# Four places in the lead-in of a graph attention kernel: tables, norms, a list of edges and an average are emitted later

## The chip, the cores and the metric

The kernel runs on one core of one Trainium2 chip. The metric is device time in microseconds (us) of one execution, as the median of several runs. A core has TensorE (matmul; the profile writes PE, and PEld for its weight loads), VectorE (DVE), ScalarE (ACT), GpSimd (POOL) and SyncE (SP, which here only issues DMAs). Each engine works through its own list of instructions in order; semaphores make one wait for another.

## The reference

A layer of graph attention with a residual and a layer norm. There are 16 batches of 1024 rows of 512 numbers, one adjacency matrix for all, 8 heads of 64. Cut to what matters:

```
q = x @ Wq + bq;  k = x @ Wk + bk;  v = x @ Wv + bv      # split in 8 heads
scores = q . k / sqrt(64) + (1 - adj) * -1e9
out = softmax(scores) . v;  y = layernorm(x + out @ Wo + bo)
```

`adj` is 0 or 1 and sparse: a row has an edge to few others, and low row numbers have many more than high ones. A row without any edge gets the mean of all v, since all its scores are then equally low.

## The kernel before, in words

**Rows are sorted by their number of edges.** In a lead-in the kernel ranks the 1024 rows, and then treats them in eight tiles of 128. For each tile it gathers, key by key, the row of k and v of each query's own next key (a "block", 128 queries by one key), so nothing is computed for absent edges. A tile t has OWN[t] blocks of that sort. Tiles 6 and 7, the rows with most edges, have besides BLOCKS[t] blocks of packed surplus edges, which a matmul with a 0/1 matrix (`sums`) adds to their queries. The function `edges(t)` makes the list of a tile's surplus: it gathers the tile's rows of `adj` (L635, on GpSimd, 128 by 1024, `codes`), multiplies them with the numbers of the places (L640), takes the greatest eight again and again (L659, L661), computes offsets through a matmul (L676), and looks for the list's entries by matmuls with 0/1 matrices (L701 to L724). `REST_FROM` says at which place of the schedule each starts.

**Tables of merged tiles.** From batch 2 on, the rows with fewest edges of two batches share one tile. `more_ranks` loads the tables for those, called `others`, by 19 small DMAs on SP (L539, L543), computes from them the rows asked for and their keys on VectorE (L552 to L578), and then squares Wq by heads on ScalarE (L583), for a bound that a final check uses. `lookups` turns keys into places, one small gather on GpSimd a step (L596), and reads the keys of `others` last.

**The fronts.** For each pair of tiles of each batch the fronts compute q, k and v from x. x is gathered (L1004), transposed (`pxT`, L751), copied by ScalarE (`xT`), and multiplied with Wq (`pq`, L793) and, in a scheme of Strassen's kind with seven products for eight, with the blocks of Wk and Wv (L950; `x`, `pp`, `z`). VectorE and ScalarE put the parts together: `e` (L963), `w` (L966), `g` (L969), k and v (L829, L973, L978, L982), `q` (L824). SP writes q, k and v to DRAM, from where GpSimd gathers them by rows. When all of a batch's v are there, `add_v` has summed them (`vsum`, L854 and L857) and `mean_pe` multiplies the sum by 1/1024 (`pm`, L861); ScalarE copies the row and SP writes it behind the batch's rows (L867). Only after that are the batch's k and v gathered.

**Attention.** For block n: gather of k and v (`kvg`, L1263), product with q (`qk`, L1284) and its sums by heads (`s`, L1288) on VectorE, exponential (L1299) and weighing of v (L1312) on ScalarE, adding up on VectorE (L1328) or TensorE (`sum`). A finished tile is divided by its sum, transposed (`poT`), multiplied with Wo (`po`), gets residual and layer norm, and is scattered to the output.

**The order is written out by hand.** One loop runs over places n, from −39 (the lead-in) to the last block, and emits the instructions for all engines. At place n it emits the product for block n + 4, gathers up to block n + 8, what was put off until n by `later` (`plan`), then what `later_last` put off, then TensorE's units as a budget of time ("credit") allows (2.0 us a place from −13 to −1, before that 3.3), and at the end one piece of each running preparation (`prep`: generators, each `yield` of which ends a place). In that part a unit of the fronts comes first, then what is in `urgent`, then more units. `edges(7)` starts at −24, `lookups` at −17, `more_ranks` at −12, `edges(6)` at −9, `bias_setup` at −8. PSUM tiles named `fill` have four buffers, shared by `pq`, `pp`, `pxT`, `pm`, `poT`, `po` and the preparations. `bias_setup` brings the biases into place (L396 to L405), adds bv times Wo to bo (`pb`, L419 and L421), and takes the greatest norms of bk and bq (L408 to L414), which are needed only by the check, at the start of the last batch.

```
if 0 <= n + 4 < total:
    products(n + 4)
...
for fn in plan.pop(n, ()):
    fn()
...
preps += prep.pop(n, [])
preps = [g for g in preps if next(g, True) is None]
```

Of the kernel before, what the change touches and what calls it, by code (L numbers as in the profile page):

```python
# [10 lines left out]
F32 = mybir.dt.float32  # L11
# [3 lines left out]
OP = mybir.AluOpType  # L15
# [16 lines left out]
KG_BUFS, Q_BUFS, QT_BUFS, PV_BUFS, Y_BUFS = 8, 5, 3, 5, 6  # L32
# [26 lines left out]
ADJ_AT = {-36: (0,), -35: (1, 2), -34: (3, 4), -33: (5,), -32: (6, 7)}  # L59
CHECKS_AT = -27  # L60
BIAS_AT = -8
MORE_RANKS_AT = -12
LOOK_FROM = -17
REST_FROM = {7: -24, 6: -9}

PRODUCT = 0.86
SUM = 0.87
# [6 lines left out]
P = 128  # L74
# [103 lines left out]
def kernel(  # L178
# [36 lines left out]
    nc = tc.nc  # L215
    B, N, D = x.shape
    HD = D // HEADS
    NPAIR = D // P
# [22 lines left out]
    W = {}  # L241
# [3 lines left out]
    bo_bc = const.tile([P, D], F32, name="bo_bc")  # L245
    flag = const.tile([1, 1], I32, name="flag")

    def broadcast(t, v):
        nc.scalar.dma_start(t, bass.AP(tensor=v.tensor, offset=v.offset, ap=[[0, P], [1, D]]))
# [4 lines left out]
    with ExitStack() as main:  # L254
        one = main.enter_context(tc.tile_pool(name="one", bufs=1))
        work = main.enter_context(tc.tile_pool(name="work", bufs=1))
# [4 lines left out]
        def fill_psum(name):  # L261
            return psum.tile([P, HALF], F32, tag="fill", name=name, bufs=4)
# [67 lines left out]
        def kv_of(b):  # L330

            if b < PAIRED_FROM:
                return solo_rows[b], 0
            rows = pair_views[b // 2 % 2][b % 2]
            return (rows, N + 1) if b % 2 else (rows[0:N + 1, :], 0)
# [58 lines left out]
        def bias_setup():  # L394
            pb = fill_psum("pb")
            nc.tensor.transpose(pb[:, 0:2 * NPAIR], bias_rows, ident[:2 * NPAIR, :2 * NPAIR])  # L396
            nc.tensor.transpose(pb[:, 2 * NPAIR:3 * NPAIR], bv_rows, ident[:NPAIR, :NPAIR])
            bk_bc = work.tile([P, D], F32, tag="y", name="bk_bc", bufs=Y_BUFS)
            broadcast(bk_bc, bk)
            yield  # L400
            nc.vector.tensor_copy(bias_qk, pb[:, 0:2 * NPAIR])
            bv_col = one.tile([P, NPAIR], F32, name="bv_col")
            nc.vector.tensor_copy(bv_col, pb[:, 2 * NPAIR:3 * NPAIR])
            bvb = work.tile([P, NPAIR, P], F32, tag="y", name="bvb", bufs=Y_BUFS)
            nc.vector.tensor_copy(bvb, bv_col[:, :, None].to_broadcast([P, NPAIR, P]))  # L405
            yield
            n4 = small.tile([P, NPAIR], F32, name="bk_norms", bufs=1)
            nc.vector.tensor_tensor(bk_bc, bk_bc, bk_bc, op=OP.mult)  # L408
            nc.vector.tensor_reduce(n4, bk_bc.rearrange("p (h d) -> p h d", d=P), axis=AX.X, op=OP.add)
            nc.vector.tensor_reduce(bk_norm, n4, axis=AX.X, op=OP.max)  # L410
            n8 = small.tile([P, HEADS], F32, name="bq_norms", bufs=1)
            nc.vector.tensor_tensor(bk_bc, bq_bc, bq_bc, op=OP.mult)
            nc.vector.tensor_reduce(n8, bk_bc.rearrange("p (h d) -> p h d", d=HD), axis=AX.X, op=OP.add)
            nc.vector.tensor_reduce(bq_norm, n8, axis=AX.X, op=OP.max)  # L414
            for _ in range(4):
                yield
            pb = fill_psum("pb3")
            for c in range(NPAIR):
                nc.tensor.matmul(pb, bvb[:, c, :], W["o"][:, c, :], start=(c == 0), stop=(c == NPAIR - 1))  # L419
            yield  # L420
            nc.vector.tensor_tensor(bo_bc, pb, bo_bc, op=OP.add)  # L421

        def bias_pieces():

            r = work.tile([P, D], F32, tag="y", name="bo_rest", bufs=Y_BUFS)
            nc.vector.tensor_copy(bo_3, bo_bc)
            nc.vector.tensor_tensor(r, bo_bc, bo_3, op=OP.subtract)
            yield  # L430
            nc.vector.tensor_copy(bo_3[32:33, :], r[32:33, :])
            nc.vector.tensor_copy(bo_3[64:65, :], r[64:65, :])
            nc.vector.tensor_tensor(r[64:65, :], r[64:65, :], bo_3[64:65, :], op=OP.subtract)
            nc.vector.tensor_copy(bo_3[64:65, :], r[64:65, :])
            yield
            st = small.tile([P, 1], F32, name="two", bufs=1)
            nc.vector.tensor_tensor(st, ident[:, 0:1], ident[:, 32:33], op=OP.add)
            nc.vector.tensor_tensor(three, st, ident[:, 64:65], op=OP.add)

        now, plan, rest, urgent, known, waiting, combined = [0], {}, {}, [], [], [], []  # L440

        def later(k, fn):
            plan.setdefault(now[0] + k, []).append(fn)
# [143 lines left out]
        def lookups():  # L587
            at = NS + NK
            groups = [[NS + own[t] + i for i in range(OWN[t])] for t in range(NT)]
            groups += [[first[t] + i for i in range(BLOCKS[t])] for t in range(len(SHORT), NT)]  # L590
            groups.append(list(range(at, at + 4)))
            for i, group in enumerate(groups):
                while i >= NT and i < len(groups) - 1 and len(SHORT) + i - NT not in listed:
                    yield
                for g in group:
                    nc.gpsimd.indirect_dma_start(  # L596
                        out=found_place[:, g:g + 1], out_offset=None, in_=place_of,
                        in_offset=bass.IndirectOffsetOnAxis(ap=key_row[:, g:g + 1], axis=0), bounds_check=N, oob_is_err=False,
                    )
                    yield  # L600
                lo, hi = group[0], group[-1] + 1

                def copy(lo=lo, hi=hi):
                    if lo == at:
                        nc.vector.scalar_tensor_tensor(
                            found_place[:, at + 1:at + 3], shifts[0].to_broadcast([P, 2]), N + 1.0, found_place[:, at + 1:at + 3],
                            op0=OP.mult, op1=OP.add,
                        )
                        nc.vector.scalar_tensor_tensor(
                            found_place[:, at + 3:], shifts[1], N + 1.0, found_place[:, at + 3:], op0=OP.mult, op1=OP.add  # L610
                        )
                    nc.vector.tensor_copy(place_row[:, lo:hi], found_place[:, lo:hi])
                    looked.append(lo)

                later(3, copy)
# [3 lines left out]
        def checks():  # L619
            for t in range(NT):  # L620

                a = ADJ[t]
                nc.scalar.activation(a, a, AF.Square, bias=neg_one, scale=2.0)
                nc.scalar.activation(a, a, AF.Square, bias=neg_one, accum_out=check[:, t:t + 1])
                yield
# [184 lines left out]
        def pair(b, j):  # L810
# [21 lines left out]
            def out_v(i, p):  # L832
                nc.scalar.copy(KV[b, tt[i]][:, D:], p)
                send(i)

            def send(i):
                assert b < PAIRED_FROM or gathered[0] >= start[max(0, b // 2 * 2 - 2)]
                kv = KV[b, tt[i]]
                rows, base = kv_of(b)
                for lo, hi in ((0, LONE), (LONE + P, 2 * P)) if b and tt[i] == 0 else ((tt[i] * P - (LONE if b and tt[i] == 1 else 0), None),):  # L840
                    hi = lo + P if hi is None else hi
                    part = slice(0 if lo % P == 0 or hi - lo == P else LONE, P if hi - lo == P or lo else LONE)
                    later(1, lambda lo=lo, hi=hi, part=part: nc.sync.dma_start(rows[base + lo:base + hi, :], kv[part, :]))
                R["sent"] = R.get("sent", 0) + 1
                if R["sent"] == 2:
                    later(1, add_v)
                    if j == NT // 2 - 1:
                        later(2, lambda: urgent.append(mean_pe))

            def add_v():  # L850
                kv = [KV.pop((b, t))[:, D:] for t in tt]
# [129 lines left out]
            def out_v0():  # L981
                nc.vector.tensor_tensor(KV[b, tt[0]][:, D:], R["z"], R["w"], op=OP.add)  # L982
                send(0)
# [223 lines left out]
        start = [min(n for n, block in enumerate(blocks) if block[0] == b) for b in range(B)] + [len(blocks)]  # L1207
# [266 lines left out]
        prep = {}  # L1474
        for t, n in REST_FROM.items():
            prep.setdefault(n, []).append(edges(t))
        prep.setdefault(BIAS_AT, []).append(bias_setup())
        prep.setdefault(CHECKS_AT, []).append(checks())
        preps = [loads(), ranks()]
        prep.setdefault(start[B - 1] + 8, []).append(guard())  # L1480
        prep.setdefault(start[1], []).append(bias_pieces())
        prep.setdefault(MORE_RANKS_AT, []).append(more_ranks())
        prep.setdefault(LOOK_FROM, []).append(lookups())
        with tc.manual_schedule():
# [21 lines left out]
            while n < total or plan or rest or urgent or done or finishing or spilled or lone_tiles or not guarded:  # L1506
# [6 lines left out]
                elif n in start:  # L1513

                    b = start.index(n)
# [110 lines left out]
```

## Time and profile before

| | |
|---|---|
| median of 3 runs | 1864.6 us (1860.19 to 1864.85) |
| the profiled execution, its own time | 1867.63 us |
| its span from first to last instruction | 1865.9 us |
| busy share of the span: TensorE, VectorE, ScalarE, GpSimd | 97%, 90%, 84%, 66% |
| mean granted clock of TensorE | 0.988 |
| DMA | 553.82 MB, mean 297 GB/s |

A page of the profile gives for each engine its busy time, and for each group of instructions the line, the operation, output<-inputs by their names in the program, and the count. In a timeline a row is start, length (both us), engine, line, operation, and in brackets the idle time of that engine before it and what ended it. Rows of one line that follow each other are merged, so that "x4" is four instructions; a float32 matmul has two records. In a list of waits a row gives who waited for what: sum in us, number, longest. The granted clock is 1.00 where TensorE ran at full speed.

### The profile page before, as it was taken

Reading aid. Unit: us, or ns where it says so; the run is one execution under the profiler, and the core shown is the slowest. Engines: PE = TensorE matmul, PEld = TensorE weight load, DVE = VectorE, ACT = ScalarE, POOL = GpSimd, SP = SyncE. Lnnn points to the kernel's source line nnn. Section 1 sums busy time; section 2 is a strip of 40 time slices with the busy share of each in tenths; the row PEclk is TensorE's granted clock in tenths of the full one; section 3 lists DMA queues with packets and bytes.
Section 4 is the critical chain, followed back from the end, with each engine's and each line's share of the span. In section 5 each row is a group of like instructions: output and inputs, shape, how many; then the busy total and the mean of one; then the engine's idle time right before and its main releaser. Section 6 shows DMA issues by size and latency. Waiting matters only on the chain.

```text
span 1865.9 us, 25322 instructions
## 1 busy us (share of the span) xinstructions
PE 1812.4 (97%) x5150; PEld 879.3 (47%) x5150; DVE 1686.2 (90%) x3462; ACT 1564.6 (84%) x6184; POOL 1237.3 (66%) x1154
## 2 busy tenths in 40 slices
PE   7989999999999999999999999999999999999995
PEld 3434444454444545444444445444544444444442
DVE  6888789999989999999999999999999999997885
ACT  3627778988889898999889898999899998987785
POOL 1367775777665776767766676677766767665774
PEclk9999999999999999999999999999999999999997
DMA  7357787998888899998998988998989999889993
GB/s 283 116 174 221 234 305 244 306 333 314 314 284 300 286 325 331 329 320 304 322 332 299 341 304 306 346 317 312 342 293 320 322 350 328 306 320 315 355 307 115
DMA packets 195431, 553.82 MB, mean 297 GB/s; under 512 B 33162, under 2 KB 33182, under 8 KB 195266
## 3 DMA queue, kind: packets, MB, share of 16 engines
q0 software_dynamic: 113600, 373.64, 59.1%
q1 hardware_dynamic: 78590, 172.65, 24.8%
q10 hardware_dynamic: 3076, 5.82, 0.9%
q14 instruction: 122, 1.00, 0.2%
q8 instruction: 43, 0.70, 0.2%
HBM read 419.52 MB, written 153.51 MB: 307 GB/s over the span
## 4 chain that ended last, share of the span: by engine, by line
PE 67%; DVE 11%; ACT 7%; DMA 5%; issue 4%; POOL 1%; SPq 0%; POOLq 0%; DVEq 0%; ACTq 0%
PE po L793 16%; PE pq L793 13%; PE pp L950 12%; PE x L950 8%; PE z L950 8%; ACT pv L1312 4%; PE poT L1372 2%; PE pxT L751 2%; DVE qk L1284 2%; PE sum L1338 2%; DVE s L1288 2%; PE sum L1337 2%; DMA oTs<-spill 1%; ACT sq_k L803 1%; DMA kvg<-kv_pair,place_row 1%
## 5 line engine op out<-in xcount | busy, mean ns | idle before, releaser
L1312 ACT ACTIVATE pv<-kvg,pv 128x64 f32<-128x64 f32 x3600 | 907.4, 341 | 0.0
L1263 POOL DMA_INDIRECT kvg<-kv_pair,place_row x462 | 535.6, 1159 | 285.7 <-ACT pv L1312 85.8
L793 PE MATMUL po<-wo,oT 128*128 128x512 f32 x816 | 375.9, 598 | 0.3 <-ACT oT L1376 0.2
L793 PE MATMUL pq<-wq,xT 128*128 128x512 f32 x792 | 367.0, 594 | 2.1 <-DVE y L1102 1.8
L1288 DVE TENSOR_REDUCE s<-qk 128x8 f32<-128x512 f32 x530 | 360.0, 679 | 6.7
L1284 DVE TENSOR_TENSOR qk<-qt,kvg 128x512 f32<-128x512 f32 x434 | 296.3, 683 | 5.8 <-DMA kvg<-kv_pair,place_row 4.8
L950 PE MATMUL pp<-t,s 128*128 128x512 f32 x504 | 239.3, 597 | 4.5 <-DVE w L966 4.5
L950 PE MATMUL x<-b,xT 128*128 128x512 f32 x504 | 239.6, 598 | 0.5 <-ACT e L963 0.4
L793 PEld LDWEIGHTS po<-wo,oT 128*128 128x128 f32 x816 | 154.7, 192 | 176.4 <-issue 168.7
L1328 DVE TENSOR_TENSOR pv<-pv,pv 128x520 f32<-128x520 f32 x329 | 227.7, 692 | 3.7 <-ACT pv L1312 2.8
L793 PEld LDWEIGHTS pq<-wq,xT 128*128 128x128 f32 x792 | 147.6, 191 | 165.5 <-issue 156.0
L1004 POOL DMA_INDIRECT x<-in_x_dram,asked_row x120 | 131.9, 1099 | 83.0 <-PE pxT L751 26.5
L1128 POOL DMA_INDIRECT out_dram<-y,asked_row x129 | 147.1, 1140 | 38.8 <-issue 24.1
L1299 ACT ACTIVATE pv<-s,absent 128x8 f32<-128x8 f32 x434 | 126.9, 294 | 52.5 <-DVE s L1288 42.3
L803 ACT ACTIVATE sq_k<-kv 128x128 bf16<-128x128 f32 x512 | 150.9, 301 | 10.4 <-DVE kv L973 6.9
L950 PEld LDWEIGHTS pp<-t,s 128*128 128x128 f32 x504 | 94.8, 192 | 114.0 <-issue 104.3
L950 PEld LDWEIGHTS x<-b,xT 128*128 128x128 f32 x504 | 94.6, 192 | 107.8 <-issue 101.2
L1217 POOL DMA_INDIRECT qg<-q_rows,query_row x96 | 106.9, 1114 | 26.8 <-issue 25.7
L950 PE MATMUL z<-b,s 128*128 128x512 f32 x252 | 119.0, 594 | 2.7 <-DVE kv L978 2.7
L950 PE MATMUL z<-t,s 128*128 128x512 f32 x252 | 118.6, 593 | 0.0
L950 PE MATMUL pp<-t,xT 128*128 128x512 f32 x252 | 118.5, 592 | 0.0
L1124 ACT ACTIVATE y<-y,stats 128x512 f32<-128x512 f32 (+1 forms) x129 | 103.7, 806 | 17.4 <-DVE stats L1119 11.9
(276 smaller groups left out, 2706.5 us busy)
## 6 DMA issues: line engine op xcount, KB each, us to landing
kv_pair<-kv SPq DMA_DIRECT2D x98, 512.0 KB
q_rows<-q SPq DMA_DIRECT2D x106, 256.0 KB
qt<-q_rows SPq DMA_DIRECT2D x98, 256.0 KB
residual<-x SPq DMA_DIRECT2D x71, 256.0 KB
y<-residual SPq DMA_DIRECT2D x71, 256.0 KB
kv_rows<-kv SPq DMA_DIRECT2D x15, 512.0 KB
kvg<-kv_pair,place_row POOLq DMA_INDIRECT x462
kv_pair<-kv SPq DMA_DIRECT2D x28, 256.0 KB
```

Of the source, the lines that this page charges most:

```text
L793: nc.tensor.matmul(p, lhs(c), w[:, c, :], start=(c == 0), stop=(c == NPAIR - 1))
L803: nc.scalar.activation(sq, s[:, ts(h, P)], AF.Square, scale=scale, accum_out=sums[:, h:h + 1])
L950: nc.tensor.matmul(R[bank], l[:, ts(c, P)], right[:, c, :], start=(first and c == 0), stop=(c == 1), skip_group_check=True,)
L1004: nc.gpsimd.indirect_dma_start(out=y, out_offset=None, in_=x_rows, in_offset=bass.IndirectOffsetOnAxis(ap=asked_row[:, t:t + 1], axis=0), ...
L1128: nc.gpsimd.indirect_dma_start(out=out_rows[b, t], out_offset=bass.IndirectOffsetOnAxis(ap=rows, axis=0), in_=y, in_offset=None, element_o ...
L1217: nc.gpsimd.indirect_dma_start(out=q, out_offset=None, in_=q_rows[b % ROWS], in_offset=bass.IndirectOffsetOnAxis(ap=rows, axis=0))
L1263: nc.gpsimd.indirect_dma_start(out=KG[n], out_offset=None, in_=rows, in_offset=bass.IndirectOffsetOnAxis(ap=(place_row if b else key_row)[ ...
L1284: nc.vector.tensor_tensor(QK[n], q, KG[n][:, 0:D], op=OP.mult)
L1288: nc.vector.tensor_reduce(S[n], QK.pop(n).rearrange("p (h d) -> p h d", d=HD), axis=AX.X, op=OP.add)
L1299: nc.scalar.activation(PV[n][:, D:], S.pop(n), AF.Exp, bias=bias)
L1312: nc.scalar.activation(pv[:, ts(h, HD)], v[:, ds(D + h * HD, HD)], AF.Copy, scale=pv[:, D + h:D + h + 1])
L1328: nc.vector.tensor_tensor(PV[b, t], PV[b, t], pv, op=OP.add)
```

## The change

Four places are changed, and nothing of what is computed.

- `more_ranks` starts at place 1 instead of −12, with its 19 loads, its tables on VectorE and its squares on ScalarE.
- The norms of bk and bq leave `bias_setup` and become a generator of their own, `bias_norms`, which starts at place 18. Its load of bk is issued there by ScalarE's queue, and its six VectorE instructions come two places later. What remains of `bias_setup` keeps its places.
- `edges(6)` starts at −6 instead of −9, with its gather, and all that follows in it is three places later too.
- The average of v of the first batch is put in `urgent` three places after its last v instead of two.

```
-MORE_RANKS_AT = -12
+MORE_RANKS_AT = 1
+NORMS_AT = 18
 LOOK_FROM = -17
-REST_FROM = {7: -24, 6: -9}
+REST_FROM = {7: -24, 6: -6}
...
         def bias_setup():
...
-            bk_bc = work.tile([P, D], F32, tag="y", name="bk_bc", bufs=Y_BUFS)
-            broadcast(bk_bc, bk)
             yield
             nc.vector.tensor_copy(bias_qk, pb[:, 0:2 * NPAIR])
...
             nc.vector.tensor_copy(bvb, bv_col[:, :, None].to_broadcast([P, NPAIR, P]))
+            yield
+            for _ in range(4):
+                yield
+            pb = fill_psum("pb3")
+            for c in range(NPAIR):
+                nc.tensor.matmul(pb, bvb[:, c, :], W["o"][:, c, :], start=(c == 0), stop=(c == NPAIR - 1))
+            yield
+            nc.vector.tensor_tensor(bo_bc, pb, bo_bc, op=OP.add)
...
+        def bias_norms():
+
+            bk_bc = work.tile([P, D], F32, tag="y", name="bk_bc", bufs=Y_BUFS)
+            broadcast(bk_bc, bk)
+            yield
             yield
             n4 = small.tile([P, NPAIR], F32, name="bk_norms", bufs=1)
             nc.vector.tensor_tensor(bk_bc, bk_bc, bk_bc, op=OP.mult)
...
             nc.vector.tensor_reduce(bq_norm, n8, axis=AX.X, op=OP.max)
-            for _ in range(4):
-                yield
-            pb = fill_psum("pb3")
-            for c in range(NPAIR):
-                nc.tensor.matmul(pb, bvb[:, c, :], W["o"][:, c, :], start=(c == 0), stop=(c == NPAIR - 1))
-            yield
-            nc.vector.tensor_tensor(bo_bc, pb, bo_bc, op=OP.add)
...
                     if j == NT // 2 - 1:
-                        later(2, lambda: urgent.append(mean_pe))
+                        later(2 if b else 3, lambda: urgent.append(mean_pe))
...
         prep.setdefault(BIAS_AT, []).append(bias_setup())
+        prep.setdefault(NORMS_AT, []).append(bias_norms())
```

## The prediction

> **What bounds the kernel now.** I read the page first, then the table by stage, then TensorE's waits, then the engines' timelines around each wait.
>
> ```profile
> PE 1812.4 (97%) x5150; PEld 879.3 (47%) x5150; DVE 1686.2 (90%) x3462; ACT 1564.6 (84%) x6184; POOL 1237.3 (66%) x1154
> ```
>
> TensorE works for 97% of 1865.9 us. The table by stage (columns: TensorE, weight loads, VectorE, ScalarE, GpSimd busy, granted clock, DMA share, GB/s) shows where the rest lies.
>
> ```profile
> 50.00:100.00 50.00, 48.72 (x128) 22.23 (x127) 42.45 (x129) 28.44 (x73) 21.96 (x21) 1.00 0.32 107
> 100.00:150.00 50.00, 40.99 (x105) 18.43 (x104) 38.15 (x104) 20.47 (x88) 29.25 (x28) 0.83 0.63 201
> 150.00:200.00 50.00, 50.00 (x142) 23.85 (x141) 43.81 (x96) 36.85 (x156) 34.38 (x33) 1.00 0.67 210
> ```
>
> After 150 us TensorE is full in nearly every stage up to 1550. So what it loses at 100 to 150, where the edits take work away, is lost at the end. TensorE's waits in 98 to 150 are three:
>
> ```profile
> PE pp L950 <- DVE w L966: 4.5, 1, 4.5
> PE pm L861 <- DVE vsum L857: 3.0, 1, 3.0
> PE pof L722 <- DVE query_row L717: 1.5, 1, 1.5
> ```
>
> TensorE's timeline (start, length, what, idle before):
>
> ```profile
> 102.07 3.60 PE L793 MATMUL pq<-wq,xT 128*128 128x512 f32 x8
> 108.72 1.02 PE L861 MATMUL pm<-vsum,mean 128*1 128x512 f32 x2 [3.05 <-DVE vsum L857]
> 109.67 3.32 PE L950 MATMUL x<-b,xT 128*128 128x512 f32 x4
> ...
> 131.26 0.60 PE L722 MATMUL pof<-ident,codes 128*128 128x128 f32 x4
> 136.35 3.78 PE L950 MATMUL pp<-t,s 128*128 128x512 f32 x4 [4.49 <-DVE w L966]
> 141.59 0.45 PE L722 MATMUL pof<-ident,codes 128*128 128x128 f32 x1 [1.46 <-DVE query_row L717]
> 142.05 6.49 PE L419 MATMUL pb<-wo,bvb 128*128 128x512 f32 x8
> 148.38 1.04 PE L751 MATMUL pxT<-ident,x 128*128 128x128 f32 x8
> ```
>
> Four matmul records of this shape follow each other in 1.72 us elsewhere (123.28 to 125.00, say), and eight in 3.43. Behind the first hole four take 3.1, behind the second `pb`'s eight take 6.3: the clock is halved after each hole, and the price of a hole is more than its idle time.
>
> [...] 3.05 us of idle was enough, and the granted clock read 0.50 from 111 to 113 us. [...] `w` waits behind whatever was emitted ahead of it. [...] the trace has one that was waited for, tile 7's adjacency rows[...]:
>
> ```profile
> 70.38 1.01 POOL L635 DMA_INDIRECT codes<-in_adj_dram,asked_row  x1 [6.25 <-ACT adj L623]
> ```
> ```profile
> 76.01 1.22 DVE L640 TENSOR_TENSOR codes<-codes,place 128x1024 f32<-128x1024 f32 x1 [0.69 <-DMA codes<-in_adj_dram,asked_row]
> ```
>
> 5.6 us from the start of the issue. I use that.
>
> **First hole (average of v).** From the end of `pq` (102.07 + 3.43 = 105.5) to the next `pxT` (114.90) lie 9.4 us; warm, the work in it is `pm` 0.95 + `x` 1.72 + `pp` 1.72 = 4.4. Lost: 5.0. VectorE ends `vsum` at 108.66, and nothing in the change moves that. One place later, `pm` stands behind that `x` and `pp`, which wait for nothing: 105.5 + 3.44 = 108.95, after `vsum`. The hole closes, all 5.0 us return, and `pxT` starts at 109.9. VectorE's own 5.01 us wait for that `pp`, before `g` (115.10), goes too: `g` runs at about 110.0.
>
> **The gathers.** GpSimd's first gather of k and v waits for the average's row in DRAM:
>
> ```profile
> 103.19 1.07 POOL L635 DMA_INDIRECT codes<-in_adj_dram,asked_row  x1 [0.30 <-issue]
> 104.69 0.96 POOL L1217 DMA_INDIRECT qt<-q_rows,asked_row  x1 [0.43 <-issue]
> 115.47 1.00 POOL L1263 DMA_INDIRECT kvg<-kv_rows,key_row  x1 [9.81 <-DMA others<-order]
> ```
>
> The row's write was issued at 113.42 on SP, behind 15 loads of the tables (106.48 to 112.92), though ScalarE had it at 110.34; the gather began 2.05 later. With the tables gone from there: `pm` 108.95, copied by 110.6, gather at 112.65, 2.8 us sooner. Its step doesn't change (−8), since the average still comes out by −9.
>
> **Second hole (w).** VectorE's work ahead of `w` (135.62) from `g` on loses, by the rows: tables 2.2 (122.44 to 124.63) + 1.3 (125.90 to 127.17) us; norms 2.9 (128.30 to 131.32); tile 6's codes 1.1 + 1.2 + 1.2 (L640, L659, L661), which come three places later. Sum 9.9, and 5.0 earlier from the first hole: `w` is ready near 121, where TensorE needs it at 131.70 − 5.0 = 126.7. The hole closes. So does the third: L717 comes by 126.4 (`qk` 1 waits for its gather until about 122, then `s` and 2.7 us of the second list) and `pof` is due at 128.4. From 131.70 to 148.38 are 16.7 us for `pp` 1.72, `pof` 0.11 and `pb` 3.43, so 11.4 lost. All of both holes: 16.4 us, and TensorE would reach the next `pxT` at 132.0 instead of 148.38.
>
> **A new hole, from the list three places later.** It issues one gather (1.07 us + 0.3 on GpSimd) and is now behind the first gathers of k and v. From the first gather to the end of step −6 GpSimd took 115.47 to 128.28; from 112.65, with 1.06 idle of which I leave the half, tile 6's gather starts at 125.4 and lands at 131.0. VectorE reaches L640 at 126.4 and stops 4.6 us, with behind it: L640 1.1, `qk`, `s`, a copy, `q` 2.1, L659 and L661 2.4, `qk` and `s` 1.3, `g` 0.6. `g` ends at 138.6. The second of the two `pxT`s of that pair needs a PSUM buffer that `g` (with `q`, the only two ready) frees: 138.6 instead of 148.82. Gain there 10.2; TensorE has then idled over 6 us and pays the slow clock once, as behind the first hole 1.8 us ((3.1 − 1.72) + 0.4). **Net gain 8.4 us.** Bounds: [...] 7.7 us, which is the most I can read (a gather of 369.64 waited for until 377.35), takes 2.1.
>
> **What is moved, and its cover.** All taken at nothing; the other end behind each. SP's 19 table loads (7.8 us of issue) go to steps 1 to 3, about 152 to 165 us, ahead of writes of q and k,v that the second batch reads no sooner than step 26; SP issued seven transfers in 150 to 178. Uncovered: a PSUM buffer waits for a `q` buffer, 5 us; excluded as likely because two are there. ScalarE's eight squares (8 × 0.6 = 4.9 us) go to steps 8 to 11, about 180 to 195, where ScalarE idles 4.05 + 0.27 + 2.31 = 6.6 us; uncovered 2. VectorE's tables (3.5 us) go to steps 6 and 7, 172 to 181, with 2.4 idle just before and in it; `w` at 185.22 is read 3.9 later, so 1.1 over is free; uncovered 1 to 3. Norms (2.9) at step 20 fall before 239.35, where VectorE idles 4.78; the bk load is issued by ScalarE two steps ahead. TensorE's matmuls are the same. A gain from the moves themselves is not excluded by ScalarE's share before step 0 (4.9 us less), but TensorE doesn't wait there.
>
> Against its own time: 1867.6 − 8.4 = 1859.2 for the profiled execution. That was 3.0 over the median, so the median goes from 1864.6 to 1856.2.
>
> **Rivals.**
> 1. *No hole at step −1.* GpSimd is quicker, or `pxT` finds another buffer: then the next limit is the gather for `qk` 3, 126.8 + 5.6 = 132.4, `g` at 134.3[...]. Gain 14.5: 1850.1. For it: 0.7 us was all tile 7 waited. Against: that list's gather had three steps with little else on GpSimd; here GpSimd has 4 us in each.
> 2. *GpSimd paces the first steps.* It has 3.9 us a step from −8 to 0 against about 2 of TensorE's share, and gathers 3 to 7, at 126.8, 131.6, 134.7, 137.8, 141.8, landing 5.6 later, cap the gain at 11.0, 12.0, 10.3, 13.5, 13.6. With landings at 7.7 the cap is 8.2 and a second hole with its 1.8 us follows: 8.4 − 2.1 − 1.8 = 4.5, 1860.1.
> 3. *Slower: GpSimd stops ahead of tile 6's gather.* The x gather of step −6 stands before it; one such waited 13.4 us (at 90.05) for a `pxT`. As long a stop delays the list and every later gather: 8.4 − 13.4 − 1.8 = −6.8, 1871.4. It decides from a stop of 6.6 on (8.4 − 1.8), and past 0.3% from 12.2. Against: here the transposes that free the buffer are done at 110.8, and the wait was 1.06.
>
> **How the numbers follow.** About 0.3%, 5.6 us, is what a measurement of this kernel can tell from no change. My forecast, gains of 5.6 to 11: 0.50. Rival 1: 0.18. Rival 2, with what else ends within 5.6 either way: 0.22. Rival 3 and its like: 0.10. Faster 0.68, same 0.22, slower 0.10. The range, 1850 to 1864.5, leaves out rival 3, the best end of rival 1 (about 0.05) and the worst of rival 2 (about 0.05). The forecast's own range is 1853.6 to 1859.0.
>
> **What would show it.** `pm` with no wait and the first gather near 112.7 (first hole). No TensorE wait for `w` or `query_row`, full clock up to about 132 (second). VectorE's L640 waiting some 4.6 us for tile 6's codes, and TensorE idle before a `pxT` that ends on `g`, then clock 0.5 for about 4 us (new hole). If L640 doesn't wait, rival 1; if `qk` of steps 0 to 4 waits for gathers, rival 2; a long GpSimd wait before step −6's x, rival 3. New TensorE waits at 165 to 195 us for ScalarE or VectorE would show that the moved work isn't covered, and would make me wrong, as would a stall elsewhere that takes the lead back.

## The result and the profile after

The changed kernel takes 1854.9 us, the median of 7 runs (1852.71 to 1859.34), against 1864.6 us for the kernel before on the same chip (7 runs, 1859.89 to 1866.18). The ratio is 0.9959, with a 95% interval of 0.9949 to 0.9970: 0.41% faster, which is 7.6 us by the ratio and 9.7 us by the medians. The predicted time was 1856.2 us, the predicted range 1850 to 1864.5.

The profiled execution of the changed kernel took 1859.34 us, with a span of 1857.6 us, and so lies 4.5 us over its own median. The profile before lay 3.0 us over its median. The two profiles are therefore read for where time went, and the medians for how much.

Line numbers shift in the changed kernel: what stood at L419 is at L410, and what stands behind it in the file is 6 higher than before (L640 is L646, L751 is L757, L950 is L956).

The page's line of busy time says that the work is the same:

```profile
PE 1807.5 (97%) x5150; PEld 878.6 (47%) x5150; DVE 1686.4 (91%) x3462; ACT 1565.1 (84%) x6184; POOL 1247.5 (67%) x1154
```

The table by stage of the kernel after (TensorE, weight loads, VectorE, ScalarE, GpSimd busy, granted clock, DMA share, GB/s) shows what has gone from the stage that lost time:

```profile
100.00:150.00 50.00, 46.41 (x133) 21.44 (x132) 42.60 (x96) 22.55 (x94) 32.67 (x31) 1.00 0.66 206
150.00:200.00 50.00, 49.85 (x144) 23.88 (x143) 45.99 (x116) 43.94 (x187) 39.51 (x35) 1.00 0.79 254
```

Between 100 and 150 us TensorE now issues 133 records instead of 105, and its clock is 1.00 instead of 0.83. The moved squares and tables are in 150 to 200 us now (ScalarE 43.94 instead of 36.85, VectorE 45.99 instead of 43.81), and TensorE there lost 0.15 us. TensorE's waits from 98 to 260 us in the kernel after:

```profile
PE pxT L757 <- ACT sums L730: 1.7, 1, 1.7
PE z L956 <- DVE kv L984: 1.1, 1, 1.1
PE pb L410 <- ACT sums L730: 0.8, 1, 0.8
PE pxT L757 <- DVE bk_norms L424: 0.6, 1, 0.6
PE pxT L757 <- DVE q L830: 0.2, 1, 0.2
```

The three waits of before (`w` 4.5, `vsum` 3.0, `query_row` 1.5) are gone, and so is a fourth, 1.8 us for a `y` at 240 us, which lies behind the stretch that the prediction reads. Five others have come, 4.4 us together. TensorE's timeline (start, length, what, idle before):

```profile
102.93 3.60 PE L799 MATMUL pq<-wq,xT 128*128 128x512 f32 x8
...
109.89 1.02 PE L867 MATMUL pm<-vsum,mean 128*1 128x512 f32 x2
110.84 1.09 PE L757 MATMUL pxT<-ident,x 128*128 128x128 f32 x8
...
130.47 3.70 PE L410 MATMUL pb<-wo,bvb 128*128 128x512 f32 x8 [0.79 <-ACT sums L730]
134.01 0.60 PE L757 MATMUL pxT<-ident,x 128*128 128x128 f32 x4
136.34 0.66 PE L757 MATMUL pxT<-ident,x 128*128 128x128 f32 x4 [1.74 <-ACT sums L730]
...
144.93 1.98 PE L956 MATMUL z<-b,s 128*128 128x512 f32 x4 [1.06 <-DVE kv L984]
```

`pm` waits for nothing. `pb`'s eight records (four matmuls) take 3.5 us (130.47 to 134.01), where they took 6.3. What the second `pxT` waits for is read from the timeline of all engines in the same stretch:

```profile
125.92 0.96 POOL L641 DMA_INDIRECT codes<-in_adj_dram,asked_row  x1 [0.30 <-issue]
129.85 0.56 ACT L730 COPY sums<-pof 128x512 f32<-128x512 f32 x1
130.18 1.23 DVE L646 TENSOR_TENSOR codes<-codes,place 128x1024 f32<-128x1024 f32 x1 [3.47 <-DMA codes<-in_adj_dram,asked_row]
132.76 0.30 ACT L1305 ACTIVATE pv<-s,absent 128x8 f32<-128x8 f32 x1 [2.35 <-DVE s L1294]
136.05 0.24 ACT L730 COPY sums<-pof 128x128 f32<-128x128 f32 x1
137.16 0.68 DVE L975 TENSOR_TENSOR g<-pp,w 128x512 f32<-128x512 f32 x1
```

Tile 6's gather starts at 125.92 and VectorE's product with it, L646, at 130.18, after a wait of 3.47. `s` of the next block stands behind L646, and so ScalarE's exponential waits until 132.76. Behind that come the weighing and four squares, and only then the copy of the last `sums`, which sets a PSUM buffer free for the second `pxT`. `g`, to which the prediction gave this part, runs after that `pxT` has begun.

**One measure for all kernels.** I take the stretch of TensorE's timeline from the start of the `pq` near 102 us (eight records) to the start of the `z<-b,s` behind the two `pxT`, the `z` and the `pq` that follow `pb`. It holds the same matmuls in every kernel, but for one small `poff` of 0.14 us that comes later where the list of edges does. A late start of an execution drops out of it. Before it runs from 102.07 to 156.26, which is 54.19 us; after from 102.93 to 144.93, which is 42.00 us. The profiles differ in it by 12.2 us.

### The profile page after: what moved, and what is told of

Its sections match the earlier page's. It is cut to its first block, busy times and chain, and to the rows that moved or that the text cites. A ratio compares the mean times of both kernels' runs of the same rounds, so it can differ in the third digit from the quotient of the medians.

```text
span 1857.6 us, 25324 instructions
## 1 busy us (share of the span) xinstructions
PE 1807.5 (97%) x5150; PEld 878.6 (47%) x5150; DVE 1686.4 (91%) x3462; ACT 1565.1 (84%) x6184; POOL 1247.5 (67%) x1154
## 4 chain that ended last, share of the span: by engine, by line
PE 69%; DVE 11%; ACT 8%; DMA 4%; issue 3%; POOL 1%; SPq 0%; POOLq 0%; DVEq 0%; ACTq 0%
PE po L799 17%; PE pq L799 14%; PE pp L956 12%; PE x L956 8%; PE z L956 8%; ACT pv L1318 5%; DVE qk L1290 2%; PE poT L1378 2%; PE pxT L757 2%; DMA kvg<-kv_pair,place_row 2%; DVE s L1294 2%; PE sum L1344 2%; PE sum L1343 2%; ACT sq_k L809 1%; DVE pv L1334 1%
## 5 line engine op out<-in xcount | busy, mean ns | idle before, releaser
L956 PE MATMUL x<-b,xT 128*128 128x512 f32 x504 | 237.1, 593 | 0.3 <-ACT e L969 0.2
L956 PE MATMUL pp<-t,s 128*128 128x512 f32 x504 | 237.0, 593 | 0.0
L956 PEld LDWEIGHTS pp<-t,s 128*128 128x128 f32 x504 | 94.3, 190 | 107.6 <-issue 98.4
L956 PEld LDWEIGHTS x<-b,xT 128*128 128x128 f32 x504 | 94.1, 190 | 106.2 <-issue 98.4
L956 PE MATMUL z<-b,s 128*128 128x512 f32 x252 | 119.0, 595 | 3.7 <-DVE kv L984 3.7
L956 PE MATMUL z<-t,s 128*128 128x512 f32 x252 | 118.6, 593 | 0.0
L956 PE MATMUL pp<-t,xT 128*128 128x512 f32 x252 | 118.5, 593 | 0.0
```

The lines of the kernel that those rows point to most:

```text
L956: nc.tensor.matmul(R[bank], l[:, ts(c, P)], right[:, c, :], start=(first and c == 0), stop=(c == 1), skip_group_check=True,)
```

## The experiments

**Each edit alone, added to the kernel before.** Four runs on one chip, on which the kernel before took 1864.57 us.

```
e1: -  later(2, lambda: urgent.append(mean_pe))
    +  later(2 if b else 3, lambda: urgent.append(mean_pe))
e2: -  MORE_RANKS_AT = -12
    +  MORE_RANKS_AT = 1
e3: +  NORMS_AT = 18     (the norms leave bias_setup for bias_norms, as in the change)
e4: -  REST_FROM = {7: -24, 6: -9}
    +  REST_FROM = {7: -24, 6: -6}
```

> The kernel before with one edit: the average of v of the first batch is asked for one place later. Theory (holes of TensorE with their slow clock set the gain): the first hole closes and gives back its 5.0 us, w's hole stays about as long, so 5 us faster, ratio 0.9973; the first gather of k and v starts some 1 us later, since the average's row is then behind all 19 table loads on SP. Rival (the start of the gathers sets the pace): no gain, up to 1 us slower.

> The kernel before with one edit: the tables of the merged tiles start at place 1 instead of -12. Theory of holes: w comes 3.5 us sooner, 132.1 against 131.7 needed, so w's hole shrinks to about 0.4 us, the clock stays full and 10 us come back, ratio 0.9946; the first hole stays at 3 us with its slow clock. Rival 1 (start of the gathers): 2.8 us. Rival 2 (the gain goes with VectorE's time taken away ahead of w, 3.5 of 9.9 us): 4 us, ratio 0.9979.

> The kernel before with one edit: the norms of bk and bq start at place 18. Theory of holes: w at 132.7 against 131.7, a hole of 1 us [...], 9 us faster, ratio 0.9952. Rival 1 (start of the gathers): nothing, ratio 1.000. Rival 2 (in proportion, 2.9 of 9.9 us): 3.3 us, ratio 0.9982.

> The kernel before with one edit: the second list of edges starts at -6 instead of -9. Theory of holes: w's hole nearly closes, but the same 3.5 us of VectorE come back before g, which stays near 144 us, so TensorE waits there, before the next transposes; 4 us faster, ratio 0.998. VectorE does not wait for the list's gather, being late itself. Rival 1 (start of the gathers): 1.4 us slower, for the gather that now stands between those of k and v. Rival 2 (in proportion, 3.5 of 9.9 us): 4 us.

| alone | median, us | ratio to before (95%) | gain by the ratio, us | stretch, us |
|---|---|---|---|---|
| e1, average | 1860.54 | 0.9983 (0.9975 to 0.9991) | 3.2 | 48.30 |
| e2, tables | 1861.03 | 0.9985 (0.9976 to 0.9994) | 2.8 | 47.90 |
| e3, norms | 1860.10 | 0.9980 (0.9972 to 0.9988) | 3.7 | 48.26 |
| e4, list | 1860.37 | 0.9980 (0.9971 to 0.9989) | 3.7 | 48.72 |

Every edit alone gains about the same, and the four sum to 13.4 us, where the whole gives 7.6. For e1 the reading of the first hole was right: `pm` waits for nothing, and the waits behind it stay as they were. The gain, 3.2 us (1.7 to 4.7), is less than the 5.0 expected; 3.3 is what is left without the 1.7 us of slow clock that most likely only the profiled execution paid (worked out further down). e4 came as expected in size, and VectorE did not wait for its gather, but the wait before the second `pxT` (1.3 us) was for `sums` and not for `g`. For e2 and e3 I had expected far more than came, since each takes enough from VectorE's queue to close most of the hole at `w`. It did close; the next one grew in its place. TensorE's waits in 98 to 260 us with the norms moved alone:

```profile
PE pof L728 <- DVE query_row L723: 3.3, 1, 3.3
PE pm L867 <- DVE vsum L863: 2.7, 1, 2.7
PE pp L956 <- DVE w L972: 1.7, 1, 1.7
```

`w` went from 4.5 to 1.7, and `query_row`, the very next thing that TensorE needs from VectorE, from 1.5 to 3.3. With the tables moved alone it is 1.1 and 3.3. In both, `pb`'s eight records behind it take 5.2 us and not 3.43, so the slow clock is still paid once. VectorE was late for two readers in a row, and more than half of what one edit gave back to the first was asked back by the second (1.8 of 2.8 us with the norms, 1.8 of 3.4 with the tables).

One rival is not ruled out by these totals: a gain in proportion to the time taken from VectorE (4, 3.3 and 4 us for e2, e3 and e4) lies inside all three intervals. For the list and the norms it falls further down, with e11 and e12, which put 3.5 and 2.9 us of that time back at no loss that shows.

The average alone and the tables alone settle what holds back the first gather of k and v. With the average alone its row leaves TensorE by 109.9 us, yet the gather starts at 117.27; with the tables alone, the hole at `pm` still there, it starts at 112.20. It was the table loads ahead of the row on SP: with the average alone there are 19, from 106.24 to 114.43, and the row's write is issued at 114.99; with the tables alone it is issued at 110.22. That the start of the gathers sets TensorE's pace, the rival for e1 and e3, falls: their gathers started at 117.27 and 116.34, no sooner than before (115.47), and they gained as much as e2.

**Each edit undone, first set.** Three edits taken back one at a time, and one gather moved, each from the changed kernel. These ran on a chip where the kernel before took 1885.0 us (1872 to 1896).

```
e5: -  REST_FROM = {7: -24, 6: -6}
    +  REST_FROM = {7: -24, 6: -9}
e6: as e5, and in edges(t), between the gather of the rows and their product:
    -  for _ in range(3):
    +  for _ in range(3 if t == 7 else 6):
e7: -  later(2 if b else 3, lambda: urgent.append(mean_pe))
    +  later(2, lambda: urgent.append(mean_pe))
e8: -  MORE_RANKS_AT = 1
    +  MORE_RANKS_AT = -12
```

> The changed kernel with one part undone: the second list of edges starts at -9 again. Theory: VectorE's wait of 3.5 us for that list's gather goes, and with it TensorE's waits of 0.8 and 1.7 us at place -1; w comes 3.5 us later, near 125.3, still before TensorE needs it at 127.7. 2.5 us faster than the changed kernel, ratio to the kernel before 0.9945. Rival (the list has to be later because VectorE has no room before w): w's or query_row's hole opens again, 3 us or more slower than the changed kernel, ratio 0.9975 or above.

> The changed kernel, but the second list's gather is issued at -9, ahead of the first gathers of k and v, and all that VectorE does with it stays three places later. Theory (the wait is for the gather's landing, nothing else): VectorE doesn't wait there, TensorE's waits of 0.8 and 1.7 us go, 2.5 us faster than the changed kernel, ratio 0.9945. Rival (VectorE's work in these places is the limit, not the landing): the waits stay, ratio as the changed kernel's, 0.996.

> The changed kernel with one part undone: the average of v is asked for two places later as before. Theory: the first hole is back, 5.0 us with its slow clock; TensorE then comes later to place -1, where the 2.5 us of waits go, so 2.5 to 5 us slower than the changed kernel, ratio 0.9972 to 0.9986. Rival (start of the gathers): no difference, as the row of the average is written as early as now.

> The changed kernel with one part undone: the tables start at -12 again. Theory: w is still in time (125.3 against 127.7), but the row of the average is behind the 19 loads on SP again, so the first gather and the list's gather start some 3 us later, and VectorE's wait for the list grows to 6 us or so; TensorE's hole at place -1 is 5 to 6 us, with the slow clock: 4 to 5 us slower than the changed kernel, ratio 0.998. Rival (only VectorE's time ahead of w counts): no difference, 0.996.

The ratios to before are 0.9990 (0.9970 to 1.0011), 0.9992 (0.9975 to 1.0008), 0.9997 (0.9979 to 1.0015) and 0.9982 (0.9963 to 1.0001). None of these totals decides anything, because all four lead-ins carry stops that belong to no edit. The average and the tables were not undone again elsewhere, so what each is worth within the change stays unmeasured. ScalarE's timeline in e6:

```profile
138.92 0.59 ACT L835 COPY kv<-x 128x512 f32<-128x512 f32 x1 [14.75 <-remote]
```

ScalarE stood for 14.75 us before a copy whose input was ready at about 127 us, and no instruction of the core released it ("remote" in the profile). In e7 there is one of 15.34 us at the same copy, e8 two of 6.05 and 6.00, and e5 one of 6.4 before an `xT`. TensorE waited 10.5 us at `pb` behind it, 11.1 in e7 and 12.3 in e8. What it waited for stays open, and whether the kernel before stops there too on that chip was not profiled. What lies ahead of the stop can be read. In e7 the hole at `pm` is back, 2.7 us. In e8 the first gather of k and v starts at 118.02 instead of 113.61, and `w` is still in time, but `pof` waits 2.5 us for VectorE; the product with tile 6's rows waits 2.5 us, where I expected 6. In e5 the product with tile 6's rows waits for nothing, and `query_row` is late instead, by 1.63 us. Even this part is to be taken with care: in e6 `query_row` is late by 1.48 us, and in e9, the same kernel on another chip, it is not late at all.

**The same again, with the changed kernel beside it.** Four runs on one chip, where the kernel before took 1861.92 us. e10 is the changed kernel, e9 is the kernel of e6, e11 that of e5; e12 is the change with the norms in their old place.

```
e12: -  NORMS_AT = 18     (the norms stay in bias_setup; the other three edits are in)
```

> The changed kernel itself, as the measure for the three others on this chip. Both theories: 7.6 to 9.7 us less than the kernel before. Its trace should repeat the three small TensorE waits that the first trace showed ahead of 150 us: pb for ScalarE's sums (0.8), the second pxT for sums (1.7), z for VectorE's kv (1.1).

> The change, with tile 6's list of edges started at -9 again but its multiplication and all behind it left three places later: only the gather of the tile's rows is early. My theory (VectorE's 3.47 us wait for that gather is what delays s, and so ScalarE's exp and sums copy, and so pb and the second pxT): VectorE's multiplication does not wait, TensorE's two waits of 0.8 and 1.7 for sums are gone, and the kernel is 2.5 us faster than the changed one, ratio to it 0.9987. Rival (the lead is lost again at the next z for kv, or at 909 us): the two waits are gone but the time is that of the changed kernel within 1 us.

> The change, with the list of edges at its old place (-9). My theory: no wait for tile 6's gather, but the list's VectorE work is ahead of w again, and TensorE waits about 1.6 us at the transposition of codes for query_row and pays the slow clock (pb 5.4 instead of 3.7, 1.7 us); against that the 2.5 us of waits for sums go: the kernel is 0 to 2 us slower than the changed one. Rival (the edits add up, each by itself worth what it gave alone): 4.2 us slower than the changed one.

> The change, with the norms of bk and bq in their old place in bias_setup. My theory (with the first hole closed, the tables gone and the list later, VectorE has spare time ahead of w, so 2.9 us of norms are covered there): w is in time, TensorE waits for it under 1 us, and the 0.6 us wait at 224 us is gone: within 1.5 us of the changed kernel. Rival (the edits add up): 4.5 us slower than the changed one, with a wait for w or query_row back.

| | median, us | ratio to before (95%) | mean, against e10 (95%), us | stretch, us |
|---|---|---|---|---|
| e10, changed | 1855.83 | 0.9961 (0.9945 to 0.9976) | | 41.88 |
| e9, gather early | 1852.97 | 0.9941 (0.9926 to 0.9956) | −3.2 (−5.6 to −0.9) | 39.86 |
| e11, list back | 1853.78 | 0.9949 (0.9935 to 0.9963) | −1.3 (−3.2 to 0.9) | 41.85 |
| e12, norms back | 1854.01 | 0.9955 (0.9941 to 0.9970) | −0.9 (−2.7 to 1.1) | 42.00 |

The intervals against e10 come from resampling the 5 or 6 runs of each, so they are rough. e10 repeats the three waits of the first trace (0.8, 1.6 and 1.1 us).

*Gather early.* VectorE's product follows `query_row` with no wait, and TensorE's rows are:

```profile
130.40 3.70 PE L410 MATMUL pb<-wo,bvb 128*128 128x512 f32 x8 [0.79 <-ACT sums L730]
133.94 1.04 PE L757 MATMUL pxT<-ident,x 128*128 128x128 f32 x8
```

The eight transpositions run in one piece. The wait of 1.6 that e10 has there is gone, which shows its chain: gather, VectorE, `s`, ScalarE's queue, the copy of `sums`, PSUM buffer, `pxT`. The stretch is 2.0 us shorter than in e10, and the kernel 3.2 us faster by the means, though the near end of that interval, 0.9 us, just touches my rival (within 1 us of the changed kernel). The two profiles don't show that the lead lasts: e9 is 2.2 us ahead of e10 up to 545 us, 0.3 to 0.5 from 600 on, and 0.4 behind from 920 on. Most of that goes at one `z` near 550, where both wait 2.38 us and only e9 pays the slow clock (shown in the last section). The other wait, 0.79 at `pb`, stayed, against my expectation: it hangs on the copy of the first four `pof`, which stands on ScalarE behind a copy of `kv` and a weighing (127.38 to 129.78) that have nothing to do with the gather. This version beats the kernel before, and by these few runs the changed one too. Its next limit shows already: VectorE waits three times for gathers of k and v up to 150 us, 1.4 us together, which it does nowhere in the changed kernel.

*List back.* I expected a loss of 0 to 2 us and the rival 4.2. The rival is out. The stretch is the same, and the mean 1.3 lower, which is not to be told from no difference, nor from a loss of up to 0.9. The later list closes the hole at `query_row` and opens the ones at `sums` and `kv`. TensorE with the list back:

```profile
131.40 0.30 PE L728 MATMUL pof<-ident,codes 128*128 128x128 f32 x1 [1.64 <-DVE query_row L723]
131.86 5.40 PE L410 MATMUL pb<-wo,bvb 128*128 128x512 f32 x8 [0.16 <-ACT sums L730]
```

1.64 of idle and 1.7 of slow clock there, against 0.8 + 1.6 + 1.1 in e10. With the other three edits in, moving the list gains nothing that shows; moving its product while leaving its gather early gains 2.0 us in the lead-in.

*Norms back.* Nothing is lost. VectorE's 2.9 us of norms are ahead of `w` again, which comes at 123.78 + 0.68, before TensorE needs it at 126.80. They fill time in which VectorE would have waited: L640's wait for tile 6's rows is 0.88 instead of e10's 3.34, and the releases behind it come as late as with the norms gone. TensorE's wait of 0.8 for `bk_norms` at about 226 us is gone with it, but `pxT` there waits for the gather of x (0.4) and for `q` (0.2) in its place.

## Why the prediction was right or wrong

**First hole: right.** `pm` waits for nothing. `pxT` starts at 110.84 in an execution that was 0.86 later at `pq` already, so 109.98 against the predicted 109.9. How much of it counts in the median is another matter, below.

**The gathers: right.** The first starts at 113.61, less 0.86 is 112.75, against 112.65. Tables alone and average alone confirm that SP's queue was the cause.

**Second and third hole: right in the whole, wrong in what each edit is worth.** `w` starts at 121.77 (120.9 without the late start, predicted near 121), L723 ends at 126.71, and `pof` at 129.41 waits for nothing. The prediction closed both by a sum of 9.9 us taken from VectorE. Less would have been enough: e12 has the 2.9 us of norms and closes both. But by itself none of the edits does.

**New hole: the step that failed.** That tile 6's gather would come too late was right: predicted start 125.4, measured 125.92 (125.06 without the late start). Three terms behind it were off. Landing: 4.3 us from the start of the issue to L646, not 5.6, so VectorE waited 3.47 and not 4.6. In e10 and e12 it is 4.1 and 4.3, while tile 7's gather of the same size took 5.6 in the profiles of before (70.38 to 76.01) and after (70.94 to 76.50). One gather was taken to stand for another, and why they differ is open. Releaser: the prediction allowed only `g` and `q` to set a buffer free, and so had the second `pxT` wait until `g` ended at 138.6; the copy of `sums` set one free at 136.3. Idle time: over 6 us in one piece, with the slow clock to pay, was predicted; there were 0.8, 1.7 and 1.1 us apart, with `pb`'s 3.5 us of work between the first two, and the clock read 1.00 in every slice from 126 to 150 us. So the profiles differ by 12.2 us over the stretch, where the sum said 8.4.

**What is moved: right.** TensorE has no wait in 150 to 220 us for SP's loads, for the squares or for the tables. The norms show once, 0.6 us, and without them another wait of that size stands there.

**From the profile to the median: wrong, and it hid the failed step.** I set the profile's 3.0 us over its median aside as if they lay elsewhere. Two things in the profile before are most likely that one execution's own.

The first is slow clock. From the end of `pq` to `pxT` the kernel before takes 9.4 us; with the tables or the norms alone the same hole, 2.90 and 2.70 us idle instead of 3.05, takes 7.6 and 7.4. Idle time apart, that is 1.7 us. And `pb` took 6.3 us before, but 5.2 in e1, e2 and e3, which is 1.1. Together 2.8 us.

The second lies behind the stretch, in the kernel before:

```profile
231.47 0.69 DVE L824 SCALAR_TENSOR_TENSOR q<-pq,bq_bc 128x512 f32<-128x512 f32 x1 [4.04 <-remote]
240.09 3.70 PE L793 MATMUL pq<-wq,xT 128*128 128x512 f32 x8 [1.75 <-DVE y L1102]
```

VectorE stood for 4.04 us before a `q` whose `pq` had ended at 228.0, and no instruction of the core released it. `y` comes late behind it, and TensorE waits 1.75 us. In e1 to e4, the changed kernel and e9 to e12 TensorE has no such wait up to 260 us, and the changed kernel's profile has no such stop; e1 to e4 gain 2.0 us on the kernel before at this place too.

For the changed kernel the sum is then: 12.2 us ahead at the end of the stretch, 10.8 just ahead of 240 us (of which 0.6 went at `bk_norms`), 12.9 behind it, and so up to 700 us (each record against the same one in the kernel before, the late start taken out). 12.9 − 2.8 − 2.0 = 8.1, beside 7.6 measured by the ratio and 9.7 by the medians. The parts were measured; that a median execution does without the 2.8 and the 2.0 is argued from these few executions, not shown by many.

So it was luck that the time was met: a new hole taken 3.8 us too large stood against about 4 us that I counted and that most likely did not count. That the profiled execution took 1859.34 us, where 1859.2 was forecast, is luck too: its lead falls from 12.9 us at 700 to 8.6 at 1000 us (a TensorE wait of 1.9 us for `q` at 910 is part of it), and e10, the same kernel, still has 12.5 there.

**The rivals.** *No hole at step −1* was half true: L646 did wait, but the clock stayed at 1.00 behind the holes of 0.8, 1.7 and 1.1 us that followed, and the time lies between that rival's 1850.1 and my 1856.2. Its gain counts no slow clock behind a hole of 2.3 us (132.0 to 134.3), which was not shown: in e11 the clock read 0.53 behind one of 1.64 us. *GpSimd paces the first steps* falls: no `qk` up to 150 us waits for a gather. It is what comes next, as the earlier gather shows. *GpSimd stops ahead of tile 6's gather* falls: it went from one issue to the next with 0.30 us between.

## What to carry to other kernels

When an engine is late for several readers in a row, the edits that relieve it need not add up (here 13.4 us as a sum of four, 7.6 together): the first hole closes and the next takes over, so follow the same queue to the second and third reader before pricing an edit alone. When a gather and its consumer are moved as one, ask whether only the consumer had to move: here a gather issued three places earlier than with its product was worth 2.0 us in the lead-in. And price a hole in the clock as a range, with its idle time as the lower end; the profiled execution shows one draw of it (here the same `z` behind the same 2.38 us of idle time took 1.98 us in one and 3.02 in another).

## What the runs showed of the hardware

The same hole has two prices. The granted clock behind it, and how long four records of the `pp` shape (1.72 us where the clock reads 1.00) or `pb`'s eight (3.43) took next:

| idle in the trace before | us | clock behind it | next |
|---|---|---|---|
| `pm`, before | 3.05 | 0.50 | `x`, four: 3.1 us |
| `pm`, e4 | 2.70 | 0.55 | `x`, four: 2.45 us, and `pm` 1.80 instead of 0.95 |
| `pm`, e2 | 2.90 | 1.00 | `x`, four: 1.82 us |
| `pm`, e3 | 2.70 | 1.00 | `x`, four: 1.82 us |
| `pof`, e11 | 1.64 | 0.53 | `pb`, eight: 5.2 us |
| `pof`, e4 | 2.07 | 1.00 | `pb`, eight: 3.5 us |

The table by stage for e4 at 111 to 113 us has the clock at 0.55 (third number from the end):

```profile
111.00:113.00 2.00, 2.00 (x3) 0.84 (x3) 0.06 (x1) 0.57 (x1) 0.00 (x0) 0.55 0.06 3
```

In the same table for e3, after a hole of the same 2.70 us, it is 1.00, and twice as many matmul records fit into the two microseconds:

```profile
111.00:113.00 2.00, 2.00 (x6) 0.89 (x5) 0.00 (x0) 0.97 (x4) 0.00 (x0) 1.00 0.02 1
```

One `z` near 550 us, behind the same wait for `kv`, gives the cleanest pair, e9 and then e10:

```profile
547.83 3.02 PE L956 MATMUL z<-b,s 128*128 128x512 f32 x4 [2.38 <-DVE kv L984]
```
```profile
550.94 1.98 PE L956 MATMUL z<-b,s 128*128 128x512 f32 x4 [2.38 <-DVE kv L984]
```

Behind 2.38 us of idle time this `z` takes 1.98 us in the kernel before, the changed kernel and e10, but 3.02 in e9. Behind 2.73 us it takes 1.98 in e11 and 2.85 in e12. It is fast four times and slow twice.

In these profiles the length of the idle time, between 1.6 and 3.1 us, did not tell whether the clock would fall: behind 1.64 us it fell in e11, behind 2.90 us it did not in e2. Why the same hole is paid for in one execution and not in another was not shown.

And there are stops that nothing on the core released. ScalarE stood for 6 to 15 us in the lead-in of all four executions profiled on one chip, about as long as what the whole change gains, or longer. The profile of the kernel before, where it takes about 1865 us and not 1885 as on that chip, has shorter ones: VectorE's 4.04 us above, and four of 2.5 to 4.6 us on ScalarE. The changed kernel's profile has none on these two engines. Their cause stays open.
